# The next image's norm and scores moved into the current image's round (two layers, four images, one core)

## The chip, the cores and the metric

The kernel runs on one core of a Trainium2 chip. A core has five engines that each work through their own queue in order and wait for each other through semaphores: TensorE (PE, matrix products), VectorE (DVE), ScalarE (ACT), GpSimd (POOL) and SyncE (SP, which here only starts transfers). The metric is the device time of one execution in microseconds; the median of three executions is given. All data is 32-bit floating point.

## The reference, cut to what matters

The input `x` is 4 images of 512 channels and 32 x 32 pixels. Two layers follow each other, each added to its own input:

```python
x = x + mamba(_gn(x))                 # layer 0: projections, a scan over 1024 pixels, gates
x = x + pab(_gn(x))                   # layer 1, the one that the change touches

def pab(x):                           # x: one normed batch, hw = 1024 pixels
    top    = conv1x1(x, w_top)    + b_top      # 64 channels
    center = conv1x1(x, w_center) + b_center   # 64 channels
    bottom = conv3x3(x, w_bottom) + b_bottom   # 512 channels
    s = softmax over all hw*hw of (center^T @ top)     # one softmax for each image
    a = (s @ bottom^T), its memory read as (512, 32, 32)
    return conv3x3(x + a, w_out) + b_out

def _gn(v):                           # 32 groups of 16 channels
    return (v - mean) / sqrt(var + 1e-5)       # over a group's channels and pixels
```

The images do not depend on each other. For one image the order is fixed by the data: norm, then scores and first convolution (both need only the normed image), then attention (needs both), then second convolution (needs the attention's sum), then the residual sum and the store.

## The kernel before, in words

Layer 0 is issued by a planner of its own in an order written out beforehand, and ends at about 2440 us. It leaves its result in device memory (`x1`). The change does not touch it.

Layer 1 is traced by plain Python loops and ordered by a scheduler, which fixes for each engine one static order of instructions, mostly the order in which the program gives them; an instruction that is ready much earlier by its estimate may move ahead. On the chip every engine keeps that static order: one that waits holds up all that stand behind it on its engine. The images go one after the other, with five functions for each:

- `norm(b)` loads four chunks of 128 channels as `x1t` (two transfers each, started on ACT, L1046). For each chunk, DVE takes statistics (`bn_stats`, `bn_aggr`, L229 and L230), PE averages over the groups with a small product (`pm_l`, L235), DVE forms the deviation (`gmean_l`, `gdev_l`, L236 to L239), PE averages again (`pv_l`, L241), ACT takes Ln and Exp (`grstd_l`, L219 and L220, each with a load of its activation table), and DVE writes the normed chunk into the padded image `xg` (L1052). `x1t` lies in the ring `f4`, which has three buffers for everything in it: `x1t`, `top`, `center` and later `o`.
- `scores(b, xg)` makes `top` and `center` (products `pt`, L1067, moved to SBUF by ACT, L1072 and L1079), then 16 score tiles of 128 x 512 (products `psc`, L1088, over 64 rows). ACT copies each into `st` (L1092), DVE takes its maximum (`mx`, L1093). POOL takes the maximum over partitions (L1098), ACT the exponentials (L1102), and PE and DVE the inverse of the sum (`pz`, L1108, and L1110).
- `conv3` is a 3x3 convolution in Winograd form: 96 products of 128 x 512 (L1182) over 24 transformed weight tiles of 1 MB, which SP loads one after the other from device memory (L1178) into three buffers. Its inputs are three pairs of transformed rows `rr` (one buffer): ACT scales (L1133, L1134), POOL adds (L1135, L1136, L1142, L1143, L1152, L1153), DVE combines (L1137, L1138, L1146, L1155) and forms the columns `v` (L1169 to L1172, two buffers). Results leave PSUM through ACT (`e`, L1190) and DVE (`n`, L1198) and are summed on POOL and DVE (L1202 to L1220). Names end in `_b` for the first convolution and in `_o` for the second.
- `attend` makes 64 products of 128 x 512 (`pat`, L1230) from `st` and the first convolution's result, and DVE adds them into `xg` in place (L1236).
- `finish` loads the residual into `o` (SP, L1247), transposes the second convolution's result on PE (`po`, L1254), adds on DVE (L1259) and stores (started on ACT, L1264).

The products of norm, scores, attention and finish share three PSUM buffers (`ps`); the convolution has five of its own. A matmul of this kernel shows as two records in the trace.

Of the kernel before, what the change touches and what calls it, by code (L numbers as in the profile page):

```python
# [16 lines left out]
B, C, HH, WW = 4, 512, 32, 32  # L17
# [143 lines left out]
def mamba_then_pab_kernel(  # L161
# [841 lines left out]
    with ExitStack() as l1:  # L1003
# [32 lines left out]
        def norm(b):  # L1036

            xg = xp.tile([P, NCC, HH + 2, WW + 2], F32, tag="xg", name=f"xg_{b}")
            nc.gpsimd.memset(xg[:, :, 0, :], 0.0)
            nc.gpsimd.memset(xg[:, :, HH + 1, :], 0.0)  # L1040
            nc.gpsimd.memset(xg[:, :, 1 : HH + 1, 0], 0.0)
            nc.gpsimd.memset(xg[:, :, 1 : HH + 1, WW + 1], 0.0)
            for c in range(NCC):
                t = fp.tile([P, L], F32, tag="f4", name=f"x1t_{b}_{c}")
                for h in range(NH):
                    nc.scalar.dma_start(  # L1046
                        t[:, h * T : (h + 1) * T], x1[b][h][c * P : (c + 1) * P, :]
                    )
                mean, rstd = group_stats(
                    f"l1_{b}_{c}", [[t[:, h * T : (h + 1) * T] for h in range(NH)]], ps, "ps"  # L1050
                )
                nc.vector.tensor_scalar(  # L1052
                    xg[:, c, 1 : HH + 1, 1 : WW + 1],
                    t.rearrange("p (h w) -> p h w", w=WW),
                    mean[:, 0:1], rstd[:, 0:1], ALU.subtract, ALU.mult,
                )
            return xg

        def scores(b, xg):


            top = fp.tile([PAB, L], F32, tag="f4", name=f"top_{b}")
            center = fp.tile([PAB, L], F32, tag="f4", name=f"center_{b}")
            for h in range(NH):
                pt = ps.tile([P, T], F32, tag="ps", name=f"pt_{b}_{h}")
                for c in range(NCC):
                    nc.tensor.matmul(  # L1067
                        pt, wt_sb[:, c].rearrange("p j n -> p (j n)"),
                        xg[:, c, 1 + h * HR : 1 + (h + 1) * HR, 1 : WW + 1],
                        start=(c == 0), stop=(c == NCC - 1),  # L1070
                    )
                nc.scalar.activation(  # L1072
                    center[:, h * T : (h + 1) * T], pt[PAB:P], AF.Identity, bias=bt_sb[PAB:P]
                )
                tv = top.rearrange("p (r k i j) -> p r i j k", r=4, k=2, j=TJ)
                pv = pt[0:PAB].rearrange("p (i r j k) -> p r i j k", r=4, j=TJ, k=2)
                hi = slice(h * TI // 2, (h + 1) * TI // 2)
                for r in range(4):
                    nc.scalar.activation(  # L1079
                        tv[:, r, hi], pv[:, r], AF.Identity, bias=bt_sb[0:PAB]  # L1080
                    )
            mx = spool.tile([P, 2 * NMC], F32, tag="mx", name=f"mx_{b}")
            st = []
            for m in range(NMC):
                t = xp.tile([P, L], F32, tag="st", name=f"st_{b}_{m}", bufs=NMC)
                for h in range(NH):
                    pt = ps.tile([P, T], F32, tag="ps", name=f"psc_{b}_{m}_{h}")
                    nc.tensor.matmul(  # L1088
                        pt, top[:, m * P : (m + 1) * P], center[:, h * T : (h + 1) * T],
                        start=True, stop=True,  # L1090
                    )
                    nc.scalar.copy(t[:, h * T : (h + 1) * T], pt)  # L1092
                    nc.vector.reduce_max(mx[:, 2 * m + h : 2 * m + h + 1], pt, axis=AX.X)  # L1093
                st.append(t)
            mp = spool.tile([P, 1], F32, tag="mp", name=f"mp_{b}")
            nc.vector.reduce_max(mp, mx, axis=AX.X)
            ma = spool.tile([P, 1], F32, tag="ma", name=f"ma_{b}")
            nc.gpsimd.partition_all_reduce(ma, mp, P, bass_isa.ReduceOp.max)  # L1098
            nc.vector.tensor_scalar_mul(ma, ma, -1.0)
            rs = spool.tile([P, NMC], F32, tag="rs", name=f"rs_{b}")  # L1100
            for m in range(NMC):
                nc.scalar.activation(  # L1102
                    st[m], st[m], AF.Exp, bias=ma, accum_out=rs[:, m : m + 1]
                )
            rp = spool.tile([P, 1], F32, tag="rp", name=f"rp_{b}")
            nc.vector.reduce_sum(rp, rs, axis=AX.X)
            pt = ps.tile([P, T], F32, tag="ps", name=f"pz_{b}")
            nc.tensor.matmul(pt[:, 0:1], ones, rp, start=True, stop=True)  # L1108
            rz = spool.tile([P, 1], F32, tag="rz", name=f"rz_{b}")
            nc.vector.reciprocal(rz, pt[:, 0:1])  # L1110
            return st, rz
# [111 lines left out]
        def attend(b, xg, st, rz, xb):  # L1223


            for j in range(NCC):
                for h in range(NH):
                    pt = ps.tile([P, C], F32, tag="ps", name=f"pat_{b}_{j}_{h}")
                    for m in range(NMC):
                        nc.tensor.matmul(  # L1230
                            pt, st[m][:, 2 * P * j + h : 2 * P * (j + 1) : 2],
                            xb[m // 2][:, m % 2, :],
                            start=(m == 0), stop=(m == NMC - 1),
                        )
                    img = xg[:, j, 1 + h * HR : 1 + (h + 1) * HR, 1 : WW + 1]
                    nc.vector.scalar_tensor_tensor(  # L1236
                        img, pt.rearrange("p (h w) -> p h w", w=WW), rz, img,
                        ALU.mult, ALU.add,
                    )

        def finish(b, y):

            dst = out[b].rearrange("(c p) h w -> p c (h w)", p=P)
            for j in range(NCC):
                o = fp.tile([P, L], F32, tag="f4", name=f"o_{b}_{j}")
                for h in range(NH):
                    nc.sync.dma_start(  # L1247
                        o[:, h * T : (h + 1) * T], x1[b][h][j * P : (j + 1) * P, :]
                    )
                ov = o.rearrange("p (i r j k) -> p r k i j", r=4, j=TJ, k=2)  # L1250
                for rr in range(2):
                    pt = ps.tile([P, 4, P], F32, tag="ps", name=f"po_{b}_{j}_{rr}")
                    for k in range(4):
                        nc.tensor.transpose(  # L1254
                            pt[:, k, :], y[2 * rr + k // 2][:, k % 2, j * P : (j + 1) * P], ident
                        )
                    for k in range(2):
                        o2 = ov[:, 2 * rr + k]
                        nc.vector.tensor_add(  # L1259
                            o2, o2, pt[:, 2 * k : 2 * k + 2].rearrange(  # L1260
                                "p k (i j) -> p k i j", j=TJ
                            ),
                        )
                nc.scalar.dma_start(dst[:, j, :], o)  # L1264

        for b in range(B):
            xg = norm(b)
            st, rz = scores(b, xg)
            xb = conv3(f"b{b}", xg, ub, brow[0])
            attend(b, xg, st, rz, xb)  # L1270
            finish(b, conv3(f"o{b}", xg, uo, brow[1]))


# [55 lines left out]
```

## Time and profile before

| | |
|---|---|
| time, median of three | 3738.53 us (3728.23 to 3745.75) |
| profiled execution, span | 3727.0 us |
| PE busy | 3000.1 us, 80% |
| DVE, ACT, POOL busy | 2447.7 us (66%), 1886.8 us (51%), 2086.6 us (56%) |
| granted TensorE clock, mean | 0.875 |
| layer 1, first load to end | 2440 to 3727 us |
| ends of the four first convolutions | 2597.2, 2917.1, 3235.3, 3555.3 us |
| PE busy, 2754 to 3072 us (one image) | 275.9 of 318 us |
| DVE, ACT, POOL busy there | 137.7, 45.9, 71.1 of 318 us |

The busy shares of the whole span mix two layers with different limits, so they say little of layer 1. Two views serve better: the chain of work that ended last, which is followed back from the end and tells for each moment what the end waited for, and the busy time by stretch. In the chain each line has a start, a length and the operation with its line in the kernel. In the stretches each engine has its busy time and the number of its instructions in parentheses. The granted clock is the share of its full speed at which TensorE was allowed to run.

### The profile page before, as it was taken

The numbers are of one execution on the slowest core, as the hardware profiler recorded it, in microseconds if no ns is written. First come the engines' busy times: TensorE is split into PE (matmuls) and PEld (weight loads), VectorE is DVE, ScalarE is ACT, GpSimd is POOL, SyncE is SP. The second block draws the span as 40 slices with busy tenths as digits, with TensorE's granted clock in tenths as the row PEclk, the third lists the DMA queues.
The fourth block names the chain that finished last, engine by engine and source line by source line (L and its number), as shares of the span: only waits on it lengthen the run. The fifth ranks groups of instructions, "written<-read, shape, count | busy, mean of one in ns | idle before, by whom it ended". The sixth has DMA issues, their size and how long they took to land.

```text
span 3727.0 us, 34784 instructions
## 1 busy us (share of the span) xinstructions
PE 3000.1 (80%) x11208; PEld 1735.7 (47%) x11208; DVE 2447.7 (66%) x2115; ACT 1886.8 (51%) x3567; POOL 2086.6 (56%) x1006
## 2 busy tenths in 40 slices
PE   5887688877687968678877768669879897986988
PEld 3455545554454555445554555424333442433433
DVE  4567877886899986889887787643445255344424
ACT  3478878775777785667885687421022003002100
POOL 7699877675766786576776798612221221123121
PEclk9888899898899989888988888769987996997899
DMA  7688667797667787766787788627264273635627
GB/s 223 190 283 288 222 210 256 239 317 242 209 224 242 263 295 277 234 210 221 259 278 275 246 312 282 214 105 271 90 237 172 110 267 106 236 135 192 218 75 253
DMA packets 378509, 836.38 MB, mean 224 GB/s; under 512 B 33560, under 2 KB 205848, under 8 KB 353496
## 3 DMA queue, kind: packets, MB, share of 16 engines
q1 hardware_dynamic: 367024, 816.50, 64.1%
q10 hardware_dynamic: 11304, 17.67, 1.4%
q8 instruction: 89, 1.46, 0.2%
q14 instruction: 92, 0.75, 0.1%
HBM read 726.57 MB, written 107.48 MB: 224 GB/s over the span
## 4 chain that ended last, share of the span: by engine, by line
PE 44%; DVE 20%; POOL 12%; issue 10%; ACT 7%; DMA 6%; SPq 1%; ACTq 0%; POOLq 0%; DVEq 0%
PE m_b L1182 9%; PE m_o L1182 9%; PE pat L1230 6%; DVE da L768 4%; PE po L347 4%; PE y L788 4%; POOL da L780 3%; DVE bbc L768 3%; PE psc L1088 3%; DVE u L768 2%; PE u L739 2%; POOL bbc L754 2%; DMA cbc<-bcd 2%; DVE xs L587 2%; PE pz L347 2%
## 5 line engine op out<-in xcount | busy, mean ns | idle before, releaser
L780 POOL TENSOR_TENSOR da<-da,cbc 128x1024 f32<-128x1024 f32 x256 | 609.3, 2381 | 294.3 <-DVE da L768 245.5
L725 ACT ACTIVATE sc<-dtxt,bt_sb 128x128 f32<-128x128 f32 x2048 | 633.2, 389 | 108.0 <-PE u L739 106.9
L768 DVE TENSOR_TENSOR_SCAN da<-da,u 128x1024 f32<-128x1024 f32 x256 | 582.3, 2275 | 151.0 <-PE u L739 136.8
L754 POOL TENSOR_TENSOR bbc<-dtx,bbc 128x1024 f32<-128x1024 f32 x256 | 607.7, 2385 | 108.8 <-DMA bbc<-bcd 86.2
L739 PE MATMUL u<-ident,sc 128*128 128x128 f32 x2048 | 321.0, 308 | 117.9 <-DVE da L768 63.1
L788 PE MATMUL y<-ident,bbc 128*128 128x128 f32 x2048 | 318.4, 306 | 116.9 <-DVE bbc L775 80.3
L788 PE MATMUL y<-ident,da 128*128 128x128 f32 x2048 | 321.5, 308 | 108.3 <-POOL da L780 101.6
L1182 PE MATMUL m_o<-uw_o,v_o 128*128 128x512 f32 x768 | 340.6, 606 | 56.1 <-DVE v_o L1169 56.1
L1182 PE MATMUL m_b<-uw_b,v_b 128*128 128x512 f32 x768 | 360.8, 629 | 10.5 <-DVE v_b L1169 10.5
L733 ACT ACTIVATE da<-dt,a_sb 128x1024 f32<-128x1024 f32 x256 | 290.6, 1140 | 144.8 <-PE y L788 130.1
L788 PEld LDWEIGHTS y<-ident,da 128*128 128x128 f32 x2048 | 271.4, 160 | 190.2 <-POOL da L780 151.6
L788 PEld LDWEIGHTS y<-ident,bbc 128*128 128x128 f32 x2048 | 271.1, 159 | 188.0 <-DVE bbc L775 96.2
L780 POOL TENSOR_TENSOR bbc<-bbc,cbc 128x1024 f32<-128x1024 f32 x128 | 306.2, 2392 | 92.5 <-DVE bbc L768 85.5
L739 PEld LDWEIGHTS u<-ident,sc 128*128 128x128 f32 x2048 | 272.5, 160 | 175.2 <-issue 77.5
L760 ACT ACTIVATE u<-dt,a_sb 128x1024 f32<-128x1024 f32 x256 | 284.4, 1111 | 112.0 <-DVE da L768 68.8
L768 DVE TENSOR_TENSOR_SCAN bbc<-u,bbc 128x1024 f32<-128x1024 f32 x128 | 292.0, 2281 | 53.8 <-ACT u L760 34.9
L768 DVE TENSOR_TENSOR_SCAN u<-u,bbc 128x1024 f32<-128x1024 f32 x128 | 292.1, 2282 | 38.9 <-POOL bbc L754 24.9
L347 PE MATMUL po<-gt,wpr 128*128 128x512 f32 x512 | 243.5, 628 | 33.2 <-DMA wt_sb<-in_w_center_dram 15.2
L1182 PEld LDWEIGHTS m_o<-uw_o,v_o 128*128 128x128 f32 x768 | 148.7, 195 | 247.6 <-issue 184.8
L347 PE MATMUL pz<-xt,winc 128*128 128x512 f32 x512 | 248.4, 623 | 8.9 <-ACT dt L676 4.8
L1182 PEld LDWEIGHTS m_b<-uw_b,v_b 128*128 128x128 f32 x768 | 150.2, 200 | 216.7 <-issue 199.4
L1230 PE MATMUL pat<-y_b,st 128*128 128x512 f32 x512 | 220.4, 592 | 0.0
(214 smaller groups left out, 4104.3 us busy)
## 6 DMA issues: line engine op xcount, KB each, us to landing
cbc<-bcd SPq DMA_DIRECT2D x512, 512.0 KB, 5.4
bbc<-bcd SPq DMA_DIRECT2D x256, 512.0 KB, 6.0
uw_b<-u_b SPq DMA_DIRECT2D x96, 1024.0 KB, 4.8
uw_o<-u_o SPq DMA_DIRECT2D x96, 1024.0 KB, 4.7
szd<-sz SPq DMA_DIRECT2D x32, 512.0 KB, 6.1
szl<-szd SPq DMA_DIRECT2D x32, 512.0 KB, 7.0
gd<-szl SPq DMA_DIRECT2D x32, 512.0 KB, 5.4
winc<-wind SPq DMA_DIRECT2D x56, 256.0 KB, 4.7
```

The costliest lines, as they stand in the source:

```text
L347: lambda k=k, lhs=lhs, rhs=rhs: nc.tensor.matmul(p(), lhs(), rhs(), start=(k == 0), stop=(k == n - 1)),
L725: nc.scalar.activation(sc()[:, k, :], dtxt()[:, k, :], AF.Copy, scale=bt()[:, k, s : s + 1],)
L733: lambda: nc.scalar.activation(da(), dt(), AF.Exp, scale=scale),
L739: nc.tensor.transpose(u()[:, k * P : (k + 1) * P], sc()[:, k, :], ident)
L754: "POOL", 2.35, lambda: nc.gpsimd.tensor_mul(dbx(), dtx(), b_bc()),
L760: lambda: nc.scalar.activation(da(), dt(), AF.Exp, scale=scale),
L768: lambda: nc.vector.tensor_tensor_scan(ht(), da(), dbx(), 0.0, ALU.mult, ALU.add),
L780: "POOL", 2.35, lambda: nc.gpsimd.tensor_mul(hc(), ht(), c_bc()),
L788: nc.tensor.matmul(y[h]()[:, k, :], hc()[:, at * P : (at + 1) * P], ident, start=(s == 0 and k == 0), stop=(s == NS - 1 and k == NK - 1), ...
L1088: nc.tensor.matmul(pt, top[:, m * P : (m + 1) * P], center[:, h * T : (h + 1) * T], start=True, stop=True,)
L1182: nc.tensor.matmul(m[q], v[:, q, k, c, :], w[:, c, :], start=(c == 0), stop=(c == NCC - 1 and not extra),)
L1230: nc.tensor.matmul(pt, st[m][:, 2 * P * j + h : 2 * P * (j + 1) : 2], xb[m // 2][:, m % 2, :], start=(m == 0), stop=(m == NMC - 1),)
```

## The change

The loop over the images is turned into a pipeline. The first image's norm and scores are given ahead of the loop. In the loop, the next image's norm is given right after the first convolution of the current one, and the next image's scores right after the current attention, ahead of the second convolution. It is meant to let one image's preparation run beside the other's convolutions. The functions themselves, the buffers and the amount of work stay the same: `xg` has two buffers already, and `st` has one set of eight, which the attention must have read before the next scores are written.

```diff
+        xg = norm(0)
+        st, rz = scores(0, xg)
         for b in range(B):
-            xg = norm(b)
-            st, rz = scores(b, xg)
             xb = conv3(f"b{b}", xg, ub, brow[0])
+            after = norm(b + 1) if b + 1 < B else None
             attend(b, xg, st, rz, xb)
+            if after is not None:
+                st, rz = scores(b + 1, after)
             finish(b, conv3(f"o{b}", xg, uo, brow[1]))
+            xg = after
```

## The prediction

> **What bounds the kernel now.** I read the chain that ended last first. Its shares by line are spread over both layers, so it had to be cut by stage. The change touches only layer 1, which runs from about 2440 us to the end at 3727 us, and there the chain walks image after image. This is one round of it (start us, length us, what), from the end of image 0's second convolution to the first products of image 1's second convolution:
> ```profile
> 2677.14 75.75 PE m_o L1182 x176
> 2753.68 2.36 POOL y_o L1203
> 2757.34 2.65 DMA out_dram<-o
> 2760.42 5.07 DMA o<-x
> 2765.67 1.42 DVE o L1259 x4
> 2771.57 1.28 ACT L220
> 2781.36 1.28 ACT L220
> 2787.16 2.54 POOL g_b L1142
> 2799.06 1.23 DVE v_b L1169
> 2800.28 3.46 DVE v_b L1170
> 2804.39 7.19 PE psc L1088 x8
> 2811.58 2.00 PE m_b L1182 x2
> 2828.43 5.42 PE psc L1088 x6
> 2833.84 6.24 PE m_b L1182 x8
> 2851.74 65.34 PE m_b L1182 x152
> 2917.09 54.95 PE pat L1230 x128
> 2972.89 2.52 POOL g_o L1142
> 2984.75 1.24 DVE v_o L1169
> 2986.03 8.71 PE m_o L1182 x16
> ```
> The reader is to see where the chain leaves PE. From 2752.9 to 2800.3 it runs through a store, a load, the next image's norm and the convolution's input transform: 47.4 us. It leaves PE again for 14.0 us between attention and second convolution (2972.0 to 2986.0). Elsewhere PE is the chain. Then I asked for busy time in four stretches: that gap, the score phase, the attention and the second gap (columns: stretch, its length, busy us and count for PE, PEld, DVE, ACT, POOL, then granted clock, DMA share, GB/s).
> ```profile
> 2752.50:2800.30 47.80, 21.65 (x71) 12.92 (x69) 22.97 (x53) 19.84 (x31) 13.01 (x6) 0.69 0.40 142
> 2804.40:2833.80 29.40, 29.40 (x33) 9.51 (x33) 16.54 (x20) 7.63 (x13) 1.73 (x1) 0.50 0.10 36
> 2917.00:2972.00 55.00, 55.00 (x129) 24.86 (x127) 5.95 (x8) 0.00 (x0) 2.35 (x1) 1.00 0.07 25
> 2972.00:2986.00 14.00, 0.02 (x1) 0.00 (x0) 6.81 (x5) 2.11 (x2) 10.61 (x5) 0.63 0.00 0
> ```
> No engine is full in the first gap: it is latency. The score phase is full on PE but at half clock (0.50). During the attention every other engine is nearly idle (DVE 5.95 of 55 us).
>
> **What the Trainium skill says.** *TensorE: Matmul & The Clock Gate*, Part 1, has PE at half rate after an idle window of about 3.4 us and at full rate after about 3.4 us of sustained work. The trace agrees on starts: clock 0.52 in 2784 to 2788, 1.00 from 2788. It goes further: through 2804 to 2834 PE is busy without pause and stays at 0.50; these are mostly the score products, which use 64 of 128 rows. The same page, Part 2 (step by step), says that matmuls stay in program order and only weight loads are pulled ahead. So a small matmul that waits holds the attention behind it. *ScalarE: Activation LUTs*, What ACT_TABLE_LOAD costs, gives 1.283 us a load plus a drain of 1.38; the trace has the 1.28 but the next activation 0.01 us later, so I use 1.28. *SBUF — State Buffer*, SBUF: two separate sides, says a DVE operation with two SBUF inputs and a POOL operation lock each other out. The trace agrees: L1170 takes 3.54 us beside POOL's l_o and 1.22 us alone.
>
> **The change part by part.** The built program's order on each engine shows where each moved piece lands. It removes no work; three rounds change (images 1 to 3).
>
> *Round before.* From one second convolution's end to the next: gap 47.4, then 33.6 to the end of the score phase (2833.84), 83.25 for the rest of the first convolution (to 2917.09), 54.9 attention, 14.0 gap, 85.5 second convolution (2986.03 to 3071.54): 318.7. The ends of the four first convolutions (2597.2, 2917.1, 3235.3, 3555.3) give a mean of 319.4.
>
> *Removed: the 47.4 us gap.* In the new order the input transform of the next first convolution (ACT L1133, POOL L1142, L1135, DVE L1137 to L1172) stands inside the second convolution, behind which it hides: in the same view DVE was busy 47.2 us and POOL 22.6 of the 86 from 2986 to 3072. The transform costs DVE some 11 us (3.6 + 1.2 + 1.23 + 3.5 + 1.75) and POOL 10 (4 x 2.4). So PE goes from m_o to the next m_b, with the 64 transposes of finish among the first four products. Their second half waits for POOL L1203, as before (3.2 us after the last product), with one m_b product in between; from the DVE adds of 0.35 us that free their PSUM buffers I get 5.5 us more on PE. A whole convolution without obstacle is 83.1 (85.5 less the half-clock start of m_o, 16 records in 8.7 to 10.0 us against 6.9, some 2.4). I add 2.4 for a half-clock start or late weights, since the stores, the o_3 load and three x1t loads now run beside weight loads that hold the DMA at 0.80. Together 91.0 (89 to 97).
>
> *Added: a wait at the attention.* PE's order puts the eight small matmuls of the next norm (pm_l and pv_l, L235 and L241) after the last m_b and ahead of the first pat. Statistics of three chunks are ready by then; what follows is not. x1t_3 needs the buffer of x1t_0, freed by the L1052 of chunk 0, and its bn_stats stand behind the L1052 of chunks 1 and 2, which wait for ACT. Counted from the last product: n_b 0.8, mean and deviation 1.0, pv 0.6, Ln, table and Exp 1.9, so chunk 0's L1052 ends at 5.2; ACT then issues a load, changes table (1.28), Ln, changes table, Exp at 8.9, and the same for chunk 2 at 11.95; L1052 to 12.8, two bn_stats 1.3 and the aggregate 0.2, pm 0.6, four small DVE operations 0.8, pv 0.6: 16.4 us. Image 0's norm in the trace took 15.5 from its first pm_l (2449.90) to the end of its last pv_l (2465.44), image 1's 15.3 (2769.13 to 2784.43). Queued behind are all 64 pat products, for them DVE L1236, then the second convolution. Nothing hides it, since before the attention started right at the last m_b. Bounds 14 to 20 (x1t loads landed in 2.5 to 9.9 us). After it PE starts at half clock: 2.5 more, so attention 57.4.
>
> *Moved: the scores.* The pt products (L1067, 6.9 us warm) lie in the 14.0 gap and are free; so are top and center on ACT and the first three psc. The first m_o follows at 14.1 after the attention. The fourth psc needs a PSUM buffer whose max (L1093) stands behind v_o L1169, L1170, L1171 on DVE: 3.54 + 3.55 + 0.7 after L1169, that is 21.7. In the first convolution only L1170 stood ahead. Then the same 26 psc and 6 m records follow: 23.45 + 6.0 = 29.45 at half clock, the rest of the convolution 83.25: 134.4. From below: were the clock full here, DVE with 15 us of its own work would set some 18, so 123. From above: DVE or DMA lag of 5, so 139. Exps and the all-reduce ended 13.4 us after the score phase and pz was waited for by nobody; that stays hidden.
>
> *Sum of a round:* 91.0 + 16.4 + 57.4 + 134.4 = 299.2 against 319.4: 20.2 saved, three times 61. Image 0 gets x1t loads and statistics among its score phase: 1 to 3 us lost, I take 2. The last image has neither norm nor scores after it and ends as before. 3738.5 - 61 + 2 = 3680.
>
> **The rivals.**
> 1. *All of it hides.* If statistics come early enough for the norm's small matmuls to cost PE little, a round saves the 47.4 less 5.5: 3 x 42 = 126, so 3612. For it: PE's own work in a round at full clock is some 250 us (two convolutions 166, attention 55, pt 7, 16 psc at 0.86 us 14, transposes and norm 8). Against: the order on PE, and the ACT chain of eight table loads, of which none can start ahead of the last n_b.
> 2. *The new waits take it all back.* Stall 20 instead of 16.4, start of the convolution starved for weights by 6 more, score phase 10 longer: 19.6 a round, so about 3738. For it: three weight buffers of 1 MB, each needed 3.4 us after the other. Against: every one must be at its worst.
> 3. *Slower.* As 2, and the attention starts late enough that DVE and ACT, still busy with the norm, hold the o transform too, 9 more a round: 3765. Against: after the stall the attention leaves 55 us in which DVE has 6 to do.
>
> **How the numbers follow.** My forecast 0.66, all hidden 0.16, taken back 0.11, slower 0.07. The forecast's own spread: a round from 123 + 89 + 14 + 57 = 283 to 139 + 97 + 20 + 57 = 313, with not all extremes at once 287 to 309, so 3641 to 3707. Below stands half of rival 1, above rivals 2 and 3 with 0.18 together; 3636 to 3712 leaves about 2 in 10 out. Half a per cent is 18.7 us, reached when a round saves 7. Faster 0.84 (forecast nearly whole, rival 1), same 0.09, slower 0.07.
>
> **What would show it.** In the profile after: the chain goes from m_o over po to m_b without x1t loads; PE idle between the last m_b and the first pat, about 16 us three times, put down to DVE gdev_l or mv_l; psc among m_o at about 1.0 us a record and clock 0.50; first m_o still 14 us after pat; last image unchanged. Wrong if that stall is under 8 or over 25 us, if psc runs at full clock, or if m_b waits for uw_b loads.

## The result, and the profile after

The changed kernel takes 3681.1 us (median of four, 3679.25 to 3688.82) against 3738.8 us (3728.23 to 3745.75): ratio 0.985, 95% interval 0.982 to 0.988, some 58 us saved. The forecast was 3680.

Layer 0's instructions are the same in both kernels, but in the profiled execution of the changed one layer 1 begins 12 us later (first `x1t` transfer at 2452.9 instead of 2440.9 us). So the two profiles are compared by stretches of layer 1. From its first load to the end it took 1286.1 us before and 1226.4 after: 59.7 us less.

The chain that ended last, one round of the kernel after (start, length, what), from the last product of image 0's first convolution to that of image 1's:

```profile
2612.94 2.34 DVE gdev_l L237
...
2620.93 1.28 ACT L220
...
2629.92 57.93 PE pat L1230 x128
...
2688.71 2.54 POOL g_o L1142
...
2705.30 3.47 DVE v_o L1171
...
2709.43 5.48 PE psc L1088 x6
2714.91 2.00 PE m_o L1182 x2
...
2763.06 58.65 PE m_o L1182 x136
...
2822.50 2.37 POOL y_o L1203
...
2824.91 1.31 PE po L1254 x10
2826.23 1.72 PE m_b L1182 x4
...
2834.60 76.05 PE m_b L1182 x176
```

The store, the load and the norm that stood between `m_o` and the next `m_b` are gone from the chain: `m_o` passes over 2.4 us of POOL and the transposes `po` straight to `m_b`. In exchange the norm's small operations stand between the first convolution and `pat`, and the scores stand between the attention and the bulk of the second convolution. The same round by stretches (columns as in the prediction: stretch, length, PE, PEld, DVE, ACT, POOL, granted clock, DMA share, GB/s):

```profile
2612.10:2629.90 17.80, 3.83 (x18) 3.46 (x16) 9.28 (x24) 9.09 (x12) 2.34 (x1) 0.58 0.30 105
2687.90:2709.40 21.50, 11.75 (x24) 4.17 (x22) 14.32 (x8) 7.71 (x15) 17.36 (x10) 0.79 0.00 0
2709.40:2738.90 29.50, 29.47 (x33) 9.59 (x33) 15.17 (x19) 7.62 (x13) 0.00 (x0) 0.50 0.10 36
2738.90:2821.70 82.80, 82.16 (x190) 35.94 (x191) 46.75 (x47) 14.74 (x24) 33.59 (x13) 0.98 0.82 288
2821.70:2910.70 89.00, 87.73 (x228) 39.85 (x226) 47.37 (x62) 4.87 (x7) 18.20 (x7) 1.00 0.89 331
```

Read top down: a wait of 17.8 us in which PE does 3.8 us of work, and which neither DVE nor ACT fills; 21.5 us until the scores resume; the score phase, PE full but at clock 0.50; the rest of the second convolution; and the next first convolution, no longer preceded by the 47.4 us gap. The ends of the four first convolutions are 2612.1, 2910.7, 3209.8 and 3506.8, so the rounds take 298.5, 299.1 and 297.1 (before: mean 319.4).

Two stretches are still poor: the wait, and the half clock. The experiments ask what each is made of and what it is worth.

### The profile page after: what moved, and what is told of

It reads as the page before. It is cut to its first block, busy times and chain, and to the rows that moved or that the text cites. A ratio compares the mean times of both kernels' runs of the same rounds, so it can differ in the third digit from the quotient of the medians.

```text
span 3679.3 us, 34763 instructions
## 1 busy us (share of the span) xinstructions
PE 2993.7 (81%) x11208; PEld 1733.5 (47%) x11208; DVE 2465.7 (67%) x2115; ACT 1885.5 (51%) x3567; POOL 2085.2 (57%) x1006
## 4 chain that ended last, share of the span: by engine, by line
PE 46%; DVE 20%; POOL 12%; issue 9%; ACT 7%; DMA 5%; SPq 0%; ACTq 0%; POOLq 0%; DVEq 0%
PE m_o L1182 9%; PE m_b L1182 9%; PE pat L1230 6%; PE y L788 5%; PE po L347 5%; DVE da L768 4%; POOL da L780 3%; PE u L739 3%; PE psc L1088 3%; POOL bbc L754 3%; PE pz L347 3%; DVE bbc L768 2%; PE pxm L347 2%; DVE u L768 2%; ACT sc L725 2%
## 5 line engine op out<-in xcount | busy, mean ns | idle before, releaser
L739 PE MATMUL u<-ident,sc 128*128 128x128 f32 x2048 | 318.2, 306 | 123.7 <-DVE da L768 72.7
L1182 PE MATMUL m_o<-uw_o,v_o 128*128 128x512 f32 x768 | 354.9, 622 | 23.8 <-DVE v_o L1169 23.2
L1182 PE MATMUL m_b<-uw_b,v_b 128*128 128x512 f32 x768 | 340.0, 602 | 6.1 <-DVE v_b L1169 5.1
L1230 PE MATMUL pat<-y_b,st 128*128 128x512 f32 x512 | 228.4, 609 | 0.0
```

The costliest lines, as they stand in the source:

```text
L739: nc.tensor.transpose(u()[:, k * P : (k + 1) * P], sc()[:, k, :], ident)
L1182: nc.tensor.matmul(m[q], v[:, q, k, c, :], w[:, c, :], start=(c == 0), stop=(c == NCC - 1 and not extra),)
L1230: nc.tensor.matmul(pt, st[m][:, 2 * P * j + h : 2 * P * (j + 1) : 2], xb[m // 2][:, m % 2, :], start=(m == 0), stop=(m == NMC - 1),)
```

## The experiments

All kernels compute the whole result. All but e9 are edits of the changed kernel. Each experiment was timed beside the kernel before on the same chip; there were three chips (e1 to e4, e5 to e8, e9 to e12), and the kernel before took 3737, 3737 and 3741 us on them.

| run | us | ratio (95%) | first two rounds, us | wait ahead of attention |
|---|---|---|---|---|
| the change | 3681.1 | 0.985 (0.982 to 0.988) | 298.4, 299.3 | 17.8 |
| e1 norm only | 3668.9 | 0.982 (0.980 to 0.984) | 297.8, 297.4 | 17.8 |
| e2 norm late | 3624.9 | 0.970 (0.967 to 0.973) | 276.4, 277.1 | none |
| e3 norm early | 3647.8 | 0.976 (0.974 to 0.978) | 290.0, 291.0 | none |
| e4 fourth buffer | 3669.5 | 0.982 (0.979 to 0.984) | 294.7, 296.4 | 14.4 |
| e5 scores on 128 rows | 3630.1 | 0.971 (0.968 to 0.974) | 281.3, 280.9 | 17.6 |
| e6 norm batched | 3630.5 | 0.971 (0.969 to 0.974) | 286.4, 286.9 | 4.2 |
| e7 maximum from the copy | 3623.0 | 0.970 (0.967 to 0.972) | 282.8, 283.8 | 17.9 |
| e8 late and batched | 3646.2 | 0.975 (0.973 to 0.977) | 290.9, 287.2 | none |
| e9 before, 128 rows | 3683.1 | 0.985 (0.982 to 0.987) | 305.6, 306.6 | none |
| e10 batched, 128 rows | 3572.4 | 0.955 (0.953 to 0.957) | 269.0, 267.7 | 4.2 |
| e11 late, 128 rows | 3606.3 | 0.963 (0.960 to 0.966) | 279.4, 276.3 | none |
| e12 late, batched, 128 rows | 3597.5 | 0.961 (0.958 to 0.964) | 278.1, 276.9 | none |

A round is taken here from the start of one attention to that of the next (before: 319.9 and 318.2); the third is left out, since the last image has no norm behind its first convolution. The wait is that of the first round, from the last product of the first convolution to the first `pat`. In the fourteen profiles the first `x1t` load is issued anywhere from 2435.5 us (e12) to 2470.7 us (e5), though no edit touches layer 0. So a difference of some 10 us between two times of this table is trusted only where the rounds show it too.

### Which half of the change brings the gain?

**e1** keeps the norm's move and takes back the scores'.

```diff
-        st, rz = scores(0, xg)
         for b in range(B):
+            st, rz = scores(b, xg)
             xb = conv3(f"b{b}", xg, ub, brow[0])
             after = norm(b + 1) if b + 1 < B else None
             attend(b, xg, st, rz, xb)
-            if after is not None:
-                st, rz = scores(b + 1, after)
             finish(b, conv3(f"o{b}", xg, uo, brow[1]))
```

> Only the norm is moved behind the first convolution; the next image's scores stay at the head of its own round. My theory (the gain is the removed gap of 47 us between images, less what the new places of norm and scores cost): the gap still goes, but the pt products (7 us) no longer lie in the idle stretch after the attention, and the score phase at half clock stands at the head of the first convolution; some 6 us a round worse than the change, so 3690 to 3705. Rival (the scores beside the second convolution are what pays): little of the gain is left, 3720 or more.

3668.9 us, and both expectations fail: the rounds are as long as those of the whole change. The norm's move alone brings the gain; moving the scores brings nothing measurable on top. The first convolution's input transform is ready early in e1 too, so the scores stand beside a convolution that does not wait for it. What the move hides in the pause after the attention (`pt`, 7.06 us, and three score tiles, 2.84 us) comes back in the changed kernel: PE waits 5.45 us for `mx`, and all the other score records run at clock 0.50, where in e1 a part of them runs at 1.00. In e1's image 1, eight records took 3.70 us at 1.00; the other 24 began at 2809.6 us, after pauses that added up to 1.3 us of the 9.5 before, and the clock fell. The last image's 32 records followed a dense stretch. These are the two stretches (columns as above):

```profile
2809.58:2828.29 18.71, 18.71 (x25) 7.07 (x25) 9.46 (x15) 6.45 (x11) 0.00 (x0) 0.56 0.00 0
3397.70:3411.70 14.00, 14.00 (x34) 5.62 (x33) 11.19 (x17) 9.44 (x18) 0.00 (x0) 1.00 0.35 124
```

So 24 records took 18.7 us at a mean clock of 0.56, and 32 took 14.0 us at 1.00. The last round (268.0 us from attention to attention, 279.2 in the change) is also where e1's lead over the change lies. This was the first sign that the clock decides what the scores cost. Whether the scores' move pays when they run at full clock was not tried.

### Another place for the norm

**e2** gives it after the attention, **e3** ahead of the first convolution.

```diff
             xb = conv3(f"b{b}", xg, ub, brow[0])
-            after = norm(b + 1) if b + 1 < B else None
             attend(b, xg, st, rz, xb)
+            after = norm(b + 1) if b + 1 < B else None     # e2
```

> The next norm is given behind the attention instead of ahead of it; the scores follow it. My theory (the norm's small products hold the attention up by about 18 us and let the clock fall, 20 us a round): that wait goes, and of it some 7 us come back because pt and the first psc no longer fit into the idle stretch; about 13 us a round better than the change, so 3640, range 3625 to 3665. Rival (the attention had to wait for something else anyway, or the norm's chain is only moved to another place on PE): 3675 to 3700.

> The next norm is given ahead of the first convolution, so that its small products stand among the early m_b products and not behind the last. My theory: the wait of 17.8 us ahead of the attention and the half-clock start behind it go, 20 us a round, so 3621; if the small products wait among the m_b for late x1t loads, up to 8 us a round come back (3645). Rival (the attention waits for something else then): 3675 to 3685.

e2 comes out at 3624.9, 56 us under the change and at the lower edge of the range. The shorter wait alone gives 3 x 17.8 = 53 us, less what the norm costs in its new place, and it does cost: the norm's chain stands beside the second convolution's transform, single `gdev_l` operations of 128 x 1 take 2.0 to 2.4 us there, and the first `m_o` starts 21.6 us after the attention instead of 14.1. What pays for it is the score phase. Its chain in e2:

```profile
2710.28 2.84 PE psc L1088 x6
...
2714.17 11.37 PE psc L1088 x26
```

26 records in 11.37 us are 0.44 us each; in the change six take 5.48, 0.91 each. Twelve `m_o` records and all `pt` had run densely just ahead, the clock was at 1.00 when the scores began, and with one pause of 0.67 us it stayed there. So e2 mixes two effects and does not price the wait by itself.

e3 (3647.8, close to the 3645 named for late loads) removes the wait too (`pat` starts at the last product's end), but only 8 us are gained a round: the small products now stand among the `m_b`, where PE follows a chain of the residual's load (6.55 us), the store (6.39), loads of `x1t` and table changes between 2810 and 2845 us. The small products that wait cost PE time in this place too.

### What the wait ahead of the attention is made of

**e4** gives the fourth chunk a free buffer of another ring, **e6** does that and takes the statistics of all four chunks in one call, so that Ln and Exp run once for four chunks.

```diff
-                t = fp.tile([P, L], F32, tag="f4", name=f"x1t_{b}_{c}")
+                if c == NCC - 1:                                   # e4, e6
+                    t = fp.tile([P, 2, C], F32, tag="y", name=f"x1t_{b}_{c}", bufs=6)
+                    t = t.rearrange("p k o -> p (k o)")
...
-                mean, rstd = group_stats(...)      # one call for each chunk
+            mean, rstd = group_stats(f"l1_{b}",    # e6: one call for all four
+                [[t[:, h * T : (h + 1) * T] for h in range(NH)] for t in ts], ps, "ps")
```

> As the change, but the fourth chunk of x1t lies in a free buffer of another ring, so its load and its statistics need not wait for the first chunk's buffer. If that buffer sets the wait ahead of the attention, it falls from 17.8 to some 8 us and the time to about 3650. If ACT's changes between the tables of Ln and Exp set it, with DVE's order behind them, only the two bn_stats, the aggregate and one small product go, some 3 us a round, so 3672.

> As the change, with the fourth x1t buffer and with one pass of statistics for the four chunks: two small products and one Ln and Exp an image instead of eight and four of each. My theory (ACT's table changes and DVE's order between them make the wait ahead of the attention): the wait falls from 17.8 to about 5 us, 12 us a round, and image 0's norm ends some 7 us earlier: 3681 - 36 - 7 = 3638, range 3625 to 3655. Rival (the wait has another source, such as the load of the last chunk): 3665 to 3680.

e4 shortens the wait from 17.8 to 14.4 us, as its second reading said (3669.5 against 3672): the buffer was the last step of it, not the bulk. e6 brings it to 4.2 us and the time to 3630.5, within its range. Of these 51 us about 10 come from image 0, whose norm nothing hides: from the issue of its first load to the end of its first convolution e6 takes 149.7 us, the change 159.7. What is left in e6 (chain, same columns):

```profile
2599.66 0.69 DVE n_b L1205
...
2600.46 2.34 DVE gdev_l L237
...
2603.24 0.59 PE pv_l L241 x2
2603.82 6.47 PE pat L1237 x8
```

So 3.4 of the 17.8 us were the buffer, and about 10 went with the batching; 2.3 of the last 4.2 are one DVE operation on 128 x 4 elements. Batching takes away small products and DVE operations together with the changes of table, so e6 does not price the tables alone. In the trace of the change five table loads of 1.28 us stand in the chain of this wait, 6.4 us. The score phase of e6 was untouched: 29.46 us at clock 0.50.

### What the half clock costs

**e5** gives the score products 128 rows: `top` and `center` are written twice, on partitions 0 to 63 and 64 to 127, `center` at half value, so that the sums are the same. The number of products and their size on the output side stay; ACT gets ten more copies an image.

```diff
-            top = fp.tile([PAB, L], F32, tag="f4", name=f"top_{b}")
-            center = fp.tile([PAB, L], F32, tag="f4", name=f"center_{b}")
+            top = fp.tile([P, L], F32, tag="f4", name=f"top_{b}")
+            center = fp.tile([P, L], F32, tag="f4", name=f"center_{b}")
...
+                for k in range(2):                 # the same for top
                     nc.scalar.activation(
-                        center[:, ...], pt[PAB:P], AF.Identity, bias=bt_sb[PAB:P])
+                        center[k * PAB : (k + 1) * PAB, ...], pt[PAB:P],
+                        AF.Identity, bias=bt_sb[PAB:P], scale=0.5)
```

> As the change, but top and center are written twice, one copy above the other (center at half value), so that every psc product works on 128 rows instead of 64, with the same sums. If the 64 rows keep the granted clock at half (a phase that enters at half clock cannot raise it with half the rows), the clock rises within a few us of the phase's start, the phase falls from 29.5 to some 18 us and four rounds gain some 10 each: 3640 to 3650. If pauses in the phase keep the clock down, the phase stays at 28 to 30 us and the time at 3670 to 3690.

3630.1 us, 51 less, and 10 below the range. The 26 score records that took 29.5 us together with six of `m_o` take 14.9 with eight, at full clock (stretch of e5, columns as above):

```profile
2712.20:2727.10 14.90, 14.90 (x35) 6.46 (x36) 14.76 (x20) 7.62 (x13) 0.00 (x0) 1.00 0.20 70
```

Twice the rows at half the time: the score phase did not pay for its work but for the clock. The PE timelines show when the clock came back. First the changed kernel, then e5 (start, length, operation, rows):

```profile
2701.91 2.07 PE L1182 MATMUL m_o<-uw_o,v_o 128*128 128x512 f32 x2 [3.07 <-DVE v_o L1169]
2709.43 5.48 PE L1088 MATMUL psc<-center,top 64*128 64x512 f32 x6 [5.45 <-DVE mx L1093]
```

```profile
2703.51 3.78 PE L1188 MATMUL m_o<-uw_o,v_o 128*128 128x512 f32 x4 [7.17 <-DVE v_o L1175]
2707.09 3.39 PE L1094 MATMUL psc<-center,top 128*128 128x512 f32 x6
```

In both the clock had fallen to 0.50 by 2703 us, in a pause of PE that the first `m_o` spends on the input transform (3.07 and 7.17 us, for `v_o` L1169 of the changed kernel and the same operation in e5). In e5 it was back at 1.00 some 5 us after the first `m_o` (0.65 in 2707 to 2709, 1.00 from 2709). In the changed kernel 29.5 us of unbroken score products with two `m_o` records after every six or eight did not bring it back; the dense `m_o` after them did.

The Trainium skill (*TensorE: Matmul & The Clock Gate*, Part 1) has the clock follow recent activity of the array in windows of about 3.4 us, and the rise in e5, some 5 us after the first `m_o`, agrees roughly. It does not say that products on half the rows count for less; here they held a full clock in e2 (32 records in 14 us) but did not raise a halved one.

**e9** puts the same 128 rows into the kernel before.

> The kernel before the change, with the scores' products over 128 rows instead of 64 (top and center written twice, center at half value, so that the sums are the same). If the half clock of the score phase belongs to products on 64 rows and not to the change, each of the four images loses some 14 us of its 29.4 us score phase, as in the changed kernel: 3682 (3672 to 3695). Rival: the ten more copies on ACT stand on the path here, since top is made right ahead of the first score product, and take back 3 to 5 us an image: 3695 to 3710. If the change itself made the half clock costly: 3725 to 3745.

3683.1, as the clock theory says: 13.7 us a round over the three rounds. In e5 four `m_o` records had run just ahead of the scores, in the changed kernel two, so these and not the rows might have raised the clock. e9 speaks against that. In its image 2 the clock falls again amid the scores (timeline of PE in e9, same columns):

```profile
3105.66 4.53 PE L1094 MATMUL psc<-center,top 128*128 128x512 f32 x6 [2.71 <-DVE mx L1099]
```

It is 0.50 in 3108 to 3110 and 0.98 in 3110 to 3112, and besides score products only two `m_b` records ran between. The half clock was there before the change, and removing it without any pipelining is worth as much (0.985) as the whole change.

**e7** reads the maximum from the SBUF copy `st` instead of from PSUM, so that a score tile's buffer does not wait for DVE.

```diff
...
-                    nc.vector.reduce_max(mx[:, 2 * m + h : 2 * m + h + 1], pt, axis=AX.X)
+                nc.vector.reduce_max(mx[:, m : m + 1], t, axis=AX.X)
```

> As the change, but the row maximum is read from the copy of the scores in SBUF (one operation of 1024 columns for two of 512), so that a psc buffer is free as soon as ACT has copied it, and PE does not wait for DVE, which is busy with v. My theory: the 5.5 us in which PE waits for mx go; if the clock stays full, because psc then follow each other without pause, the phase needs 14 to 17 us instead of 29.5, some 20 to 25 us a round less in all: 3590 to 3620. If 64 rows cannot hold the full clock even without pauses, 5 to 11 us a round: 3640 to 3665.

3623.0, 3 us outside the range of the clock theory and 17 below that of its rival. In PE's order all 32 score records now stand ahead of the first `m_o`, and they run at clock 1.00 (timeline of PE in e7, same columns):

```profile
2665.79 14.00 PE L1088 MATMUL psc<-center,top 64*128 64x512 f32 x32 [1.26 <-ACT top L1079]
2704.54 0.58 PE L1108 MATMUL pz<-rp,ones 128*128 128x1 f32 x2 [9.57 <-DVE rp L1106]
```

Then PE waits 9.6 us ahead of `pz` for the exponentials, which had been hidden. In the changed kernel the clock falls where the first `m_o`, placed behind three score tiles, waits 3.07 us for `v_o` (0.86 in 2699 to 2701, 0.50 from 2701); the wait for `mx` comes after that. So two pauses stood among the scores there and none in e7, and e7 does not tell them apart.

### Do the two costs add?

**e8** is e2 and e6 together; **e10**, **e11** and **e12** add 128 rows to e6, e2 and e8.

> The norm behind the attention as in e2, with the batched statistics of e6. My theory (in e2 the chain of eight small products stretched to 30 us beside the o transform and delayed m_o from 14 to 21.5 us after the attention): the chain falls to some 8 us, m_o starts at about 15 to 17 us, and a round loses another 8 to 14 us against e2: 3585 to 3605. Rival (e2's gain came from the clock alone, the length of the norm's chain does not matter any more): 3615 to 3630.

> The changed kernel with the batched norm and the fourth input buffer (3630 alone) and with the scores over 128 rows (3630 alone). The first shortens the wait ahead of the attention, the second the score phase; if the two costs are separate the gains add: 3580 (3570 to 3592). Rival: one engine, DVE or ACT, stands behind both, so that the second gain comes at half or less: 3600 to 3625.

> The next norm given after the attention (3625 alone), with the scores over 128 rows. If the late norm gained because its score products ran at full clock already, 128 rows can save only in image 0, some 14 us: 3611 (3602 to 3622). Rival: the clock had nothing to do with its gain, and 128 rows save 14 us in each round: 3570 to 3585.

> The late norm, batched, with the scores over 128 rows. Late and batched alone took 3646, more than late without batching (3625), with its score products back at half clock. If the clock was the reason, 128 rows bring it down by 14 us for each of four images: 3590 (3580 to 3602). Rival: the batched statistics beside POOL's input transform are what costs, whatever the clock: 3620 to 3645.

e8 contradicts both of its expectations: 3646.2, slower than the late norm without batching. Its chain shows the second cost:

```profile
2666.78 7.62 DVE xg L1059 x4
...
2688.20 2.07 PE psc L1095 x2
...
2692.28 5.42 PE psc L1095 x6
```

The scores are back at half clock. With the batched norm the second convolution's transform waits for four `xg`, 7.62 us in all, beside POOL, the scores' maxima stand behind the transform again, PE pauses 3.0 us, and the clock falls. e11 and e12 test that reading. e11 should gain only in image 0, whose scores alone were at half clock in e2, and gains 19 us (3606.3; four times 14 would have been 3570). e12 should regain all four; it regains 48.6 us (3597.5, within its range) and lands near e11. So the loss of e8 is a matter of the clock, and so is the larger part of e2's gain: with 128 rows in both, the late norm is worth 24 us (3630.1 to 3606.3), not 56.

e10 joins the two cures, and they add: 3572.4 against 3580 expected, 109 us under the change where the two alone give 51 each, and 166 under the kernel before. Its wait (chain of e10) and its score phase (stretch):

```profile
2590.40 2.35 DVE gdev_l L237
...
2593.77 58.03 PE pat L1243 x128
```

```profile
2674.52:2689.47 14.95, 14.95 (x35) 6.51 (x36) 14.82 (x20) 7.63 (x13) 0.00 (x0) 1.00 0.19 70
```

## Why the prediction was right, step by step

*The gap removed.* Right: from the second convolution's end to the end of the next first convolution it took 88.9, 89.9 and 88.6 us, where 91.0 stood. The 2.4 us that I had added for a half clock or late weights was hardly needed: the granted clock is 1.00 in all three, and PE waited for weights once, 1.1 us.

*The wait added.* Its place and cause were right, its size 17.8, 17.6 and 17.8 instead of 16.4. The missing term is one operation, `gdev_l`, inside the 1.0 us that I had put for mean and deviation. The timeline of the changed kernel (start, length, engine, operation, shapes, idle time before):

```profile
2612.92 2.34 POOL L1203 TENSOR_TENSOR y_b<-y_b,n_b 128x1024 f32<-128x1024 f32 x1 [11.33 <-DVE gmean_l L236]
2612.94 2.33 DVE L237 TENSOR_TENSOR gdev_l<-mv_l,gmean_l 128x1 f32<-128x1 f32 x1
...
2616.96 0.16 DVE L237 TENSOR_TENSOR gdev_l<-mv_l,gmean_l 128x1 f32<-128x1 f32 x1
```

DVE's `gdev_l` has two inputs in SBUF and starts 0.02 us after POOL's last sum of the convolution. It ends with it. For the next chunk, with POOL idle, the same operation takes 0.16 us. The prediction used the lock that it cited from the Trainium skill (*SBUF — State Buffer*, SBUF: two separate sides) for large operations only; here a small one takes as long as the POOL operation beside it. e4 confirms the buffer as the end of the term; e6 shows that the four passes one after the other are its bulk, without parting ACT's tables from DVE's order.

*The attention at a half-clock start.* 57.93, 57.23 and 57.75 instead of 57.4, and 54.95 for the last image, which has no wait ahead. In e2, where the wait is gone, all four take 54.95.

*The scores moved.* The fourth `psc` came 21.6 us after the attention (21.7 stood), the score phase took 29.5 at clock 0.50 (29.45), the rest 82.8 (83.25). As a forecast that was exact, by carrying over a phase measured before. As an explanation it was thin: I took the half clock as given, and read the moved scores as partly free. The floor of some 18 us that I gave the phase at full clock was too high: it took 14.9 (e5). e1 shows that this half of the change brings nothing, and e5, e6 and e10 that the phase held as much to gain as the wait, 51 us each.

*The round and the sum.* 298.2 us measured, 299.2 predicted; image 0's part grew by 2.9 where 2 stood. The last image ends as before. The mechanism held at each named sign; that the total fits to 1 us is in part luck, since the stretch without the gap was put 1.9 us too long and the wait 1.3 too short, and since executions of the kernel before lie up to 17.5 us apart.

*The rivals.* "All of it hides" (3612) failed on the order on PE, as argued; e10 goes below its time, but by cutting the wait and the half clock, not by better hiding. "The new waits take it all back" would have needed each at its worst; the weights, for one, cost the first convolutions only that 1.1 us in the whole of layer 1. "Slower" needed still more.

What stays open: why products on 64 rows hold a full clock but do not raise a halved one, and how many rows would do; only 64 and 128 were tried. The batched norm was not tried in the kernel before, so how much of its gain needs the pipeline is not known. And no run explains why layer 0 ends up to 35 us apart between profiles.

## What to carry to other kernels

Moving independent work ahead pays by what the chain loses, and costs where its small dependent products fall in an engine's fixed order: place them so that their inputs are long ready, or batch them (here 13.6 of 17.8 us came back). Before pipelining around a stretch in which TensorE is full, look at its granted clock: here a full engine at 0.50 was worth as much as an idle gap, and the cure may be a pause less or more rows, not another order. When two edits each gain 50 us, ask whether they cure the same cost: the late norm and batching both cured the wait and did not add up, batching and rows did.

## What the runs showed of the hardware

- Products on 64 rows, with two `m_o` records after every six or eight, ran for 29.5 us without pause at clock 0.50; with the same products on 128 rows the phase took 14.9 us at 1.00 (e5).
- Begun at 1.00 and without pauses, 32 records of products on 64 rows took 14.0 us and kept it (e7); after 9.5 us at 1.00 with 1.3 us of pauses, 24 of them took 18.7 us at a mean of 0.56 (e1).
- A DVE operation on 128 x 1 elements took 2.33 us beside a POOL operation of 2.34 us, and 0.16 us with POOL idle (the changed kernel).
